# First layer of a four-layer network: inverse norms and softmax reciprocals spread over the channels by HBM reads instead of matmuls

## The chip, the cores and the metric

One core of a Trainium2 chip runs the whole network in one launch, in float32. The engines are named as the profile names them: PE (TensorE matmuls; PEld its weight loads), DVE (VectorE), ACT (ScalarE), POOL (GpSimd) and SP (SyncE, which here issues the DMAs of this layer). The metric is the device time in microseconds (us), the median of several executions of the same program. A time is given against the profiled execution where it is read from the trace.

## What is computed

The network has four layers over x of shape (2, 512, 64, 64). The change touches the first one, attention with a 3x3 neighbourhood and pooled keys, run on the normalised input of each image. Per image there are N = 4096 tokens, C = 512 channels in 8 heads of 64. Cut to what matters:

```
q = heads(xf @ W_q + b_q)
q_norm = q / max(norm(q), 1e-12)                  # per head and token
q_scaled = (q_norm + query_embedding) * softplus(temperature)
k_l, v_l = split(xf @ W_kv + b_kv)
k_l = k_l / max(norm(k_l), 1e-12)                 # per head and token
k_local, v_local = the 9 neighbours (3x3, zero padded) of k_l, v_l
attn_local = sum over channels of q_scaled * k_local        # 9 per head and token
attn_pool  = q_scaled . l2norm(k_pool)                      # 256 pooled keys
a_local, a_pool = split(softmax(concat(attn_local, attn_pool)))
lt = q_norm . learnable_tokens + learnable_bias + a_local
out = (sum over 9 of lt * v_local + a_pool . v_pool) @ W_proj + b_proj
```

Two quantities exist once per head and token and must multiply all 64 channels of the head: the inverse norm of k and q, and the reciprocal of the softmax's sum (on the pooled part; `lt` for the nine neighbours carries it already). The channels lie on the partitions, so each has to be spread over 64 partitions. How that is done is what the change changes.

## The kernel before

`Net.layer0` opens the pools and runs the class `Local`: SBUF `wp`, DRAM `yp`, and PSUM with five banks for `mm` (the method `bank`), one for `tap` and two for `qs`. Work is cut into units. A unit is 1024 tokens (16 rows of the image, two blocks of 512) of one chunk of 128 channels (two heads); 4 units by 4 chunks are 16 units an image.

`run` goes through turns i = -4 to 16. In turn i it makes generators and interleaves them step by step (`in_turn` takes one step of each in a round):

- `norms`: the inverse norms of what was projected in the turn before. Four matmuls sum the squares of four streams (k and q, two blocks each) over the heads (L2048), ACT copies to SBUF (L2051), four transposes (L2055), small DVE operations for the inverse root (L2062 to L2070), four transposes back (L2076) and an ACT copy to `rows` (L2078).
- `tap_products(i+1)`: two ACT copies of the scaled queries to PSUM (L2133), then nine DVE multiplies of 128x1024, one for each neighbour, with the keys `kx` (L2138), in a ring of three buffers `prods`.
- `attend(i)`: scores against the pooled keys (L2183), exponentials on ACT (L2187), values (L2193) with an ACT copy (L2195), sums of exponentials on POOL (L2198), then the softmax's sums on PE (L2205, L2209), two DVE reciprocals of 128x256 (L2230), the multiply of `el` by them (L2233) and the addition of the learned term (L2234). The rows are written to HBM (`rows`, L2237), and read back broadcast over the channels as "taps", one per neighbour, by `fetch_tap` (L2247: two DMAs of 256 KB, one a head).
- `weigh(i-1)`: the reciprocal, spread by two K=2 matmuls (L2260), multiplies the pooled output (DVE, L2263). Then for each of nine taps: ACT copies the tap to PSUM (L2270), DVE multiplies with the values `vx` (L2273), POOL adds to the output (L2277). The result goes to HBM as `yd` (L2283). The taps have a ring of three buffers.
- `tap_sums(i+1)`: matmuls that sum each product over the head (L2151), and the exponential (ACT, L2166) which gives `el`.
- `projections`: k of unit i+4, q of unit i+3 and v of unit i+1: a block is four matmuls of 128x512, one per chunk of input channels (L133; the trace has two records for each matmul; k and q stand at the end of the steps), with ACT taking out k or q with its bias (L2014) and its square (L2016), v with its bias (L2122).
- `normed`: the spread of the inverse norms by four K=2 matmuls (L2090), DVE multiplies k into `kx` and q in place (L2098), then `learned`: four matmuls with the learned tokens (L2111), ACT adds their bias (L2114) and scales the queries (L2116).
- in the last turns `fetch_output` and `output`: the projection `W_proj`, with the reload of `yd`.

The generators give the order in which operations are written down; the framework then puts them in an order per engine and sets the waits for data and buffers. Every engine takes its instructions in that order. All DMAs of this layer are issued by SP, in order as well: a DMA that must wait for data or a buffer holds those behind it.

Quantities per turn in the middle of an image: 21 DMAs issued by SP; 18 ACT copies of taps; nine products and nine tap multiplies in two halves on DVE.

## Time and profile before

| | |
|---|---|
| median of 11 executions | 5453.23 us |
| lowest, highest | 5436.49, 5470.63 us |
| the profiled execution | 5456.72 us |
| its span | 5454.8 us, so 1.9 us lie around it |
| mean granted PE clock | 0.969 |
| instructions | 51666 |
| one turn in the middle of the first layer (9 per image) | 45.86 us |
| the nine of image 1, 446.06 to 858.78 | 412.72 us |
| the nine of image 2, 3147.28 to 3560.01 | 412.73 us |

How to read it: the span is the profiled execution from first to last instruction. A row of groups gives a line of the kernel, engine, operation, its operands by the program's names (tiles that are parts of a larger buffer carry its name: `big` and `late` hold most of this layer), the shape, how many there were, then busy time, the mean of one in ns, and the idle time of the engine just before them with what ended most of it. A row of the timeline gives start, duration, engine, line and operation, and in brackets the idle time before it with the releaser. Windows give the busy time of each engine in a stretch. A count of matmul records can be a few per cent short. The 512-column matmuls of one block L133 that follow each other show 3.70 us as a row, and the next work of PE starts 3.63 us after its start.

The change touches no line outside the first layer.

### The profile page before, as it was taken

To read this page: it belongs to the slowest core of one execution; us is meant where nothing else is said; L and a number is where in the kernel's file an instruction comes from. 1 tells how busy PE (TensorE), PEld (TensorE's weight loads), DVE (VectorE), ACT (ScalarE), POOL (GpSimd) and SP (SyncE) were. 2 spreads that over 40 slices of the span, in tenths; PEclk is the share of its full clock that TensorE was granted. 3 is DMA by queue.
4 is the path that set the end of the run, shared out by engine and by line. 5 is a ranking of instruction groups with operands and counts; after the bars stand their busy time and mean duration, and the time that the engine had idled before them with its cause. 6 is when DMAs were issued, how large, how long until landed. Compare 5 with 4: busy or idle time off the path is not lost. (4 is left out here: it accounts for less than half of the span.)

```text
span 5454.8 us, 51666 instructions
## 1 busy us (share of the span) xinstructions
PE 5161.4 (95%) x18891; PEld 2251.2 (41%) x18891; DVE 3144.1 (58%) x3918; ACT 1793.5 (33%) x3409; POOL 1802.9 (33%) x1198
## 2 busy tenths in 40 slices
PE   7999999999988899999999999998999889999998
PEld 3423333554333444544344233335543334445443
DVE  3256667745679633565532666666456895334565
ACT  1245555233212233212212555542432132332221
POOL 0025556401310045444400355553012101554443
PEclk9999999999989999899999999999999899998999
DMA  3024445500000000211110344455000000000111
GB/s 141 2 63 122 127 126 160 147 18 24 1 1 0 1 0 1 84 34 56 51 55 2 83 126 128 125 152 149 1 24 0 1 0 1 1 8 20 37 36 42
DMA packets 113564, 293.27 MB, mean 54 GB/s; under 512 B 17235, under 2 KB 30035, under 8 KB 111253
## 3 DMA queue, kind: packets, MB, share of 16 engines
q1 hardware_dynamic: 113300, 289.88, 18.4%
q8 instruction: 151, 2.47, 0.2%
q14 instruction: 113, 0.92, 0.1%
HBM read 241.32 MB, written 48.50 MB: 53 GB/s over the span
## 5 line engine op out<-in xcount | busy, mean ns | idle before, releaser
L133 PE MATMUL mm<-big,w 128*128 128x512 f32 x2560 | 1189.6, 609 | 5.0 <-DVE late L2230 4.9
L133 PEld LDWEIGHTS mm<-big,w 128*128 128x128 f32 x2560 | 468.2, 192 | 688.5 <-issue 592.5
L2277 POOL TENSOR_TENSOR late<-late,big 128x1024 f32<-128x1024 f32 x192 | 454.6, 2368 | 304.6 <-DVE big L2273 296.1
L1265 POOL TENSOR_TENSOR total<-prob 128x512 f32<-128x512 f32 x128 | 159.6, 1269 | 761.7 <-ACT prob L1262 761.7
L1182 PE MATMUL acc<-big,dg 128*128 128x512 f32 x704 | 317.5, 608 | 58.8 <-DVE big L697 28.3
L1624 POOL TENSOR_SCALAR qf_sum<-qf,ksum_ratio 128x512 f32<-128x512 f32 x128 | 198.8, 1562 | 508.9 <-ACT qf L1674 351.6
L1437 POOL TENSOR_TENSOR big<-big 128x512 f32<-128x512 f32 x224 | 277.4, 1270 | 238.5 <-ACT big L1428 238.5
L2198 POOL TENSOR_TENSOR late<-late 128x512 f32<-128x512 f32 x128 | 160.6, 1276 | 490.7 <-ACT late L2187 450.9
L697 DVE TENSOR_TENSOR big<-big 128x3968 f32<-128x3968 f32 x72 | 308.8, 4290 | 6.9 <-ACT big L698 0.9
L2273 DVE TENSOR_TENSOR big<-big,mm 128x512 f32<-128x512 f32 x384 | 254.4, 679 | 85.7 <-ACT mm L2270 82.6
L1428 ACT ACTIVATE big<-mm,ed 128x256 f32<-128x256 f32 x512 | 193.9, 488 | 279.1 <-DVE top L1424 251.4
L2270 ACT COPY mm<-big 128x512 f32<-128x512 f32 x384 | 221.1, 594 | 170.9 <-DMA big<-rows 131.9
L1362 PE MATMUL mm<-proj,k 64*128 64x256 f32 x2048 | 270.5, 394 | 0.9 <-ACT k L1329 0.9
L1282 DVE RECIPROCAL recip<-psD 128x512 f32<-128x512 f32 x64 | 214.9, 3357 | 87.2 <-PE psD L1279 87.2
L1655 PE MATMUL mm<-k,w 128*128 128x512 f32 x512 | 241.1, 610 | 14.6 <-DVE k L1648 14.6
L1583 DVE TENSOR_REDUCE tops<-mm 128x2 f32<-128x512 f32 x256 | 161.4, 684 | 160.9 <-PE mm L1362 160.4
L1262 ACT ACTIVATE prob<-mm 128x512 f32<-128x512 f32 x256 | 132.0, 605 | 364.4 <-PE mm L1259 359.2
L1362 PEld LDWEIGHTS mm<-proj,k 64*128 64x128 f32 x2048 | 207.2, 188 | 105.9 <-issue 90.1
L2138 DVE TENSOR_TENSOR prod<-qs,big 128x1024 f32<-128x1024 f32 x192 | 230.4, 1215 | 30.9 <-PE tap L2151 29.1
L2277 POOL TENSOR_TENSOR late<-late,tap 128x1024 f32<-128x1024 f32 x96 | 226.6, 2361 | 63.6 <-DVE tap L2273 44.9
L133 PE MATMUL mm<-big,big 128*128 128x512 f32 x512 | 238.8, 629 | 0.0
L2151 PE MATMUL tap<-prod,cst 128*32 128x512 f32 x768 | 226.4, 612 | 9.6 <-DVE prod L2138 9.5
(364 smaller groups left out, 8295.8 us busy)
## 6 DMA issues: line engine op xcount, KB each, us to landing
big<-rows SPq DMA_DIRECT2D x384, 256.0 KB
tap<-rows SPq DMA_DIRECT2D x192, 256.0 KB
yd<-late SPq DMA_DIRECT2D x32, 512.0 KB
lost_all<-lost SPq DMA_DIRECT2D x128, 128.0 KB
out<-big SPq DMA_DIRECT2D x64, 256.0 KB
big<-in_W_kv SPq DMA_DIRECT2D x8, 1024.0 KB
rows<-late SPq DMA_DIRECT2D x64, 128.0 KB
big<-yd SPq DMA_DIRECT2D x16, 512.0 KB
```

The source lines that it names most:

```text
L133: self.nc.tensor.matmul(ps, w[:, kc, :], X[:, kc, blk * TB:(blk + 1) * TB], start=(kc == 0), stop=(kc == KC - 1))
L697: nc.vector.tensor_tensor(o, a, b, ALU.max)
L1182: nc.tensor.matmul(accs[b], dg, src[:, b * TB:(b + 1) * TB], start=(j == 0), stop=(j == 6))
L1282: nc.vector.reciprocal(r, psD)
L1362: nc.tensor.matmul(pS[h][i][:, t, :], k[lo:lo + HD, tok:tok + P], proj[lo:lo + HD, :], start=True, stop=True)
L1437: nc.gpsimd.tensor_tensor(a, a, part, ALU.add)
L1655: nc.tensor.matmul(ps, self.wo[:, kc, oc * P:(oc + 1) * P], qs[:, kc, :], start=(kc == 0), stop=(kc == KC - 1))
L2138: self.nc.vector.tensor_tensor(self.prods[k % 3].rearrange("p (y x) -> p y x", x=W), qs, self.kx[:, y + dy:y + dy + self.UY, dx:dx + W], A ...
L2151: nc.tensor.matmul(ps[32 * q:32 * q + 32, :], self.cst[:, C_TAPW + 16 - 2 * k:C_TAPW + 48 - 2 * k], self.prods[k % 3][:, j * TB:(j + 1) * ...
L2270: nc.scalar.copy(ps, part)
L2273: nc.vector.tensor_tensor(part.rearrange("p (y x) -> p y x", x=W), self.vx[:, y:y + self.UY // 2, dx:dx + W], ps.rearrange("p (y x) -> p y ...
L2277: nc.gpsimd.tensor_tensor(out, out, self.taps[k % 3], ALU.add)
```

## The change

The reciprocals and inverse norms are no longer spread by matmuls; they are written to HBM and read back broadcast over 64 partitions each, as the taps are. In detail:

1. `norms` ends with two DMAs that write the inverse norms (8 KB each) to a DRAM tile `roots`, and four DMAs that read them back broadcast over all channels (256 KB each; queries into two of the `sq` tiles, keys into `kraw`; queries first). `normed` copies them to PSUM by ACT (four copies; in place of the K=2 matmuls L2090), and DVE multiplies as before. ACT writes k, not yet normalised, straight into `kx`, and the multiply is in place there. Queries come before keys, and `learned` right after the queries.
2. The softmax's reciprocal is read from a row of `el` (row 20 of each half), where the multiply by the reciprocal leaves it: there the exponential is exp(0) = 1, and the learned term is 0. `fetch_tap` takes it as a tenth tap with number 0; `weigh` copies it to PSUM by ACT (two copies, in place of the K=2 matmuls L2260) and multiplies the pooled output with it in its first step. The ring of taps now turns with 10u + i.
3. `norms` and `normed` stand after `projections` in the list of stages; `norms` has two steps fewer, `normed` waits six steps instead of five, `fetch_output` seven instead of three.

```diff
--- before.py
+++ after.py
@@ -1715,6 +1715,7 @@
 
         self.yd = yp.tile([P, KC, N], F32, name="yd")
         self.wd = yp.tile([3, P, KC, C], F32, name="wd")
+        self.roots = cycle([yp.tile([2, 4, TB], F32, name=f"roots{i}") for i in range(2)]).__next__
         self.rows = cycle([yp.tile([P // 2, self.UT], F32, name=f"rows{i}") for i in range(2)]).__next__
 
         R = W + 2
@@ -1749,12 +1750,13 @@
         self.vp = new([P, 2, C], "vp")
         self.qn = new([P, self.UT], "qn")
         self.w3 = new([P, 3, KC, P], "w3")
-        self.sq = [new([P, TB], f"sq{i}") for i in range(4)]
+
+        self.squares = new([P, 4, TB], "sq")
+        self.sq = [self.squares[:, i, :] for i in range(4)]
         self.half = new([P, 32], "mhalf32")
         self.wide = new([P, NT, P], "wide")
         self.qb = new([P, KC], "qe_scaled")
         self.bias = {i: new([P, KC], "b_" + i) for i in "qkv"}
-        self.raw = {"k": self.kraw, "q": self.qn}
         self.w, self.lt, self.el, self.out = {}, {}, {}, {}
         load = lambda w, src: nc.sync.dma_start(w, src.rearrange("(kc p) o -> p kc o", p=P))
         load(self.w_sr, d["W_sr"])
@@ -1791,7 +1793,7 @@
         for i in range(-4, units + 1):
             k, q, ahead, u, before = (unit(i + n) for n in (4, 3, 1, 0, -1))
             streams, ended = [], []
-            stages = [self.norms(streams, ended)]
+            stages = []
             if ahead is not None:
                 stages.append(self.tap_products(ahead))
             if u is not None:
@@ -1804,7 +1806,7 @@
             values = ([ahead] if i >= self.UN - 1 and ahead is not None
                       else {-4: [0], -3: [1, 2], -2: [3]}.get(i, []))
             stages.append(self.projections(k, q, values, streams))
-            stages.append(self.normed(ended))
+            stages += [self.norms(streams, ended), self.normed(ended)]
             if i < -2:
                 stages.append(islice(heads, 12 if i == -4 else None))
             if i == units - 3:
@@ -1945,7 +1947,7 @@
 
     def fetch_output(self):
 
-        for _ in range(3):
+        for _ in range(7):
 
             yield
         for kc in range(KC):
@@ -2010,8 +2012,13 @@
                 return
             b = self.bias[which][:, u // self.UN:][:, :1]
             ps = self.projected(which, u % self.UN * 2 + j)
-            part = self.raw[which][:, j * TB:(j + 1) * TB]
-            nc.scalar.activation(part, ps, AF.Identity, bias=b)
+            if which == "k":
+                y = 1 + u % self.UN * self.UY + j * self.UY // 2
+                part = self.kx[:, y:y + self.UY // 2, 1:W + 1]
+            else:
+                part = self.qn[:, j * TB:(j + 1) * TB]
+            nc.scalar.activation(part, ps.rearrange("p (y x) -> p y x", x=W) if which == "k" else ps,
+                                 AF.Identity, bias=b)
             sq = self.sq[len(streams)]
             nc.scalar.activation(sq, ps, AF.Square, bias=b)
             streams.append((which, u, j, part, sq))
@@ -2042,7 +2049,6 @@
         before, self.pending = self.pending, streams
         if not before:
             return
-        yield
         ps = self.bank()
         for s in range(4):
             nc.tensor.matmul(ps[32 * s:32 * s + 32, :], self.cst[:, C_E32:C_E32 + 32],
@@ -2070,40 +2076,46 @@
             nc.vector.scalar_tensor_tensor(dst, a, 1.5, y, ALU.add, ALU.mult)
         yield
         yield
-        yield
         ps = self.bank()
         for t in range(NT):
             nc.tensor.transpose(ps[:, t * P:(t + 1) * P], self.wide[:, t, :], self.net.ident)
         rows = wp.tile([P, TB], F32, name="n_rows")
         nc.scalar.copy(rows, ps)
-        ended += [(s, rows[32 * s:32 * s + 2, :], *a) for s, a in enumerate(before)]
+
+        roots = self.roots()
+        for h in range(2):
+            nc.sync.dma_start(roots[h], rows[h:P:32, :])
+        for s in reversed(range(0, len(before), 2)):
+            dst = (self.kraw if before[s][0] == "k"
+                   else self.squares[:, 2:].rearrange("p s n -> p (s n)"))
+            for h in range(2):
+                nc.sync.dma_start(dst[h * HD:(h + 1) * HD, :].rearrange("p (s n) -> p s n", s=2),
+                                  bcast(roots[h, s:s + 2], 0, HD))
+            ended += [(dst[:, j * TB:(j + 1) * TB], *before[s + j]) for j in range(2)]
         yield
 
     def normed(self, ended):
 
         nc = self.nc
-        for _ in range(5):
-            yield
-        for which in "kq":
-            mine = [(e, self.bank()) for e in ended if e[2] == which]
-            for (s, rows, *_), ps in mine:
-                nc.tensor.matmul(ps, self.cst[32 * s:32 * s + 2, C_ROW:C_ROW + P], rows, start=True,
-                                 stop=True)
-            for (_, _, _, u, j, part, _), ps in mine:
-                out = part
+        for _ in range(6):
+            yield
+        for which in "qk":
+            mine = [(e, self.bank()) for e in ended if e[1] == which]
+            for (root, *_), ps in mine:
+                nc.scalar.copy(ps, root)
+            for (_, _, u, j, part, _), ps in mine:
                 if which == "k":
-                    y = 1 + u % self.UN * self.UY + j * self.UY // 2
-                    out = self.kx[:, y:y + self.UY // 2, 1:W + 1]
-                    part, ps = (a.rearrange("p (y x) -> p y x", x=W) for a in (part, ps))
-                nc.vector.tensor_tensor(out, part, ps, ALU.mult)
-            yield
-        if mine:
-            self.learned(mine[-1][0][3])
-        yield
+                    ps = ps.rearrange("p (y x) -> p y x", x=W)
+                nc.vector.tensor_tensor(part, part, ps, ALU.mult)
+            yield
+            if which == "q":
+                if mine:
+                    self.learned(mine[-1][0][2])
+                yield
 
     def learned(self, u):
 
-        nc, cc, qn = self.nc, u // self.UN, self.raw["q"]
+        nc, cc, qn = self.nc, u // self.UN, self.qn
         ps = self.bank()
         for j in range(2):
             for g in range(2):
@@ -2235,49 +2247,47 @@
         self.spread = self.rows()
         for j in range(2):
             nc.sync.dma_start(self.spread[:, j * TB:(j + 1) * TB], el[j * HD:(j + 1) * HD, :])
-        self.fetch_tap(0)
-        yield
-        self.fetch_tap(1)
-        yield
-
-    def fetch_tap(self, k):
-
-        at = 32 * (k % 2) + 2 * k
+        self.fetch_tap(u, 0)
+        yield
+        self.fetch_tap(u, 1)
+        yield
+
+    def fetch_tap(self, u, i):
+
+
+        at = 32 * ((i - 1) % 2) + 2 * (i - 1) if i else 20
+        t = self.taps[(10 * u + i) % 3]
         for h in range(2):
-            self.nc.sync.dma_start(self.taps[k % 3][h * HD:(h + 1) * HD, :],
-                                   bcast(self.spread[at + h], 0, HD))
+            self.nc.sync.dma_start(t[h * HD:(h + 1) * HD, :], bcast(self.spread[at + h], 0, HD))
 
     def weigh(self, u):
 
         nc = self.nc
         cc, y0 = u // self.UN, u % self.UN * self.UY
-        out, R = self.out.pop(u), self.recip
-        self.fetch_tap(2)
-        yield
-        banks = [self.bank() for _ in range(2)]
-        for j, ps in enumerate(banks):
-            q = slice(64 * j, 64 * j + 2)
-            nc.tensor.matmul(ps, self.cst[q, C_ROW:C_ROW + P], R[q, :], start=True, stop=True)
-        for j, ps in enumerate(banks):
-            o = out[:, j * TB:(j + 1) * TB]
-            nc.vector.tensor_tensor(o, o, ps, ALU.mult)
-        for k in range(9):
-            dy, dx = divmod(k, 3)
-            parts = [self.taps[k % 3][:, j * TB:(j + 1) * TB] for j in range(2)]
+        out = self.out.pop(u)
+        for i in range(10):
+            if i + 2 < 10:
+                self.fetch_tap(u, i + 2)
+            t = self.taps[(10 * u + i) % 3]
+            parts = [t[:, j * TB:(j + 1) * TB] for j in range(2)]
 
             banks = [self.bank() for _ in range(2)]
             for ps, part in zip(banks, parts):
                 nc.scalar.copy(ps, part)
+            dy, dx = divmod(i - 1, 3)
             for j, (ps, part) in enumerate(zip(banks, parts)):
+                if i == 0:
+                    o = out[:, j * TB:(j + 1) * TB]
+                    nc.vector.tensor_tensor(o, o, ps, ALU.mult)
+                    continue
                 y = y0 + dy + j * self.UY // 2
                 nc.vector.tensor_tensor(
                     part.rearrange("p (y x) -> p y x", x=W),
                     self.vx[:, y:y + self.UY // 2, dx:dx + W],
                     ps.rearrange("p (y x) -> p y x", x=W), ALU.mult)
-            nc.gpsimd.tensor_tensor(out, out, self.taps[k % 3], ALU.add)
-            if k + 3 < 9:
-                self.fetch_tap(k + 3)
-            if k < 8:
+            if i:
+                nc.gpsimd.tensor_tensor(out, out, t, ALU.add)
+            if i < 9:
                 yield
         lo = u % self.UN * self.UT
         nc.sync.dma_start(self.yd[:, cc, lo:lo + self.UT], out)
```

## The prediction

> **What bounds the kernel now.** I read the page's first part (busy time by engine) first, then the busy time of each engine in windows of one turn, then the groups and the order of time within one turn.
>
> ```profile
> PE 5161.4 (95%) x18891; PEld 2251.2 (41%) x18891; DVE 3144.1 (58%) x3918; ACT 1793.5 (33%) x3409; POOL 1802.9 (33%) x1198
> ```
>
> TensorE (PE) is the engine to relieve over the whole span. The chain of waits names only about a fifth of the span and no line of this layer, so it doesn't help. The first layer is what the change touches; cut at the starts of the matmuls of L2260, each turn in its middle looks like this (time, then busy time by engine, clock, DMA share, GB/s):
>
> ```profile
> 491.91:537.77 45.86, 45.74 (x166) 14.75 (x165) 31.60 (x50) 25.85 (x45) 26.21 (x13) 1.00 0.48 126
> 537.77:583.63 45.86, 45.74 (x167) 14.75 (x165) 31.60 (x50) 25.82 (x45) 26.20 (x13) 1.00 0.46 121
> ...
> 858.78:1100.00 241.22, 223.58 (x662) 109.40 (x660) 176.46 (x271) 85.18 (x151) 126.44 (x61) 0.97 0.54 151
> 225.00:351.32 126.32, 121.33 (x406) 43.72 (x401) 46.96 (x85) 45.05 (x71) 5.01 (x4) 0.96 0.07 19
> 351.32:446.06 94.74, 87.33 (x307) 26.71 (x305) 61.72 (x100) 50.07 (x87) 52.43 (x26) 0.98 0.46 117
> ```
>
> In the nine steady turns of an image (446.06 to 858.78, and again in image 2: 18 in all) PE idles 0.12 of 45.86 us; DVE is at 69%, ACT 56%, POOL 57%. So a matmul taken away there is worth its full time as long as nothing makes PE wait, and every wait of PE costs its full length. Around them PE has holes: 5.0 us before 351.32, 7.4 in the first turns, 17.6 in the last ones.
>
> The groups of the steady turns (busy, mean ns, idle before):
>
> ```profile
> L2138 DVE TENSOR_TENSOR prod<-qs,big 128x1024 f32<-128x1024 f32 x54 | 65.0, 1216 | 12.5 <-PE tap L2151 11.7
> ...
> L2230 DVE RECIPROCAL late<-mm 128x256 f32<-128x256 f32 x18 | 30.3, 1726 | 3.7 <-PE mm L2209 3.7
> L2090 PE MATMUL mm<-n_rows,cst 2*128 2x512 f32 x72 | 20.3, 640 | 0.0
> ...
> L2263 DVE TENSOR_TENSOR late<-late,mm 128x512 f32<-128x512 f32 x18 | 12.3, 683 | 91.7 <-PE mm L2260 91.7
> ```
>
> DVE idles 10.2 us at each turn's head (91.7 over nine) until PE reaches L2260. That is slack of DVE, no loss of time: PE works through it.
>
> And the place that the change disturbs, in order of time (start, duration):
>
> ```profile
> 515.46 1.07 PE L2209 MATMUL mm<-late,cst 64*64 64x512 f32 x4
> ...
> 516.46 3.70 PE L133 MATMUL mm<-big,w 128*128 128x512 f32 x8
> 516.58 3.37 DVE L2230 RECIPROCAL late<-mm 128x256 f32<-128x256 f32 x2 [0.41 <-PE mm L2209]
> ...
> 522.05 1.23 DVE L2138 TENSOR_TENSOR big<-qs,big 128x1024 f32<-128x1024 f32 x1 [0.18 <-PE tap L2151]
> ...
> 524.98 1.22 DVE L2138 TENSOR_TENSOR prod<-qs,big 128x1024 f32<-128x1024 f32 x1
> ```
>
> After the sums DVE takes the reciprocals, and the next unit's first two tap products (L2138) start 5.6 and 8.5 us after the sums' end. PE asks for them only at 541.5 (a turn after its first tap matmuls, L2151, of 495.68), because both q blocks, scores, a v block and values stand ahead. The wait is covered.
>
> [...] a pair with K=2 (L2260, L2090) holds PE 1.05 us, a full pair of L133 0.91 (a block of eight 3.63 from start to start). [...] Here the pair of writes of the rows (issued 521.90, 1.10 us) is followed by the first read at 524.90: about 1.9 us of SP standing still. [...]
>
> **The change part by part.**
>
> *Removed.* Six K=2 matmuls a turn (four of L2090, two of L2260), three pairs of 1.055 us: 3.17 us of PE a turn. In the order that the changed program has once built, the tap matmuls also stand in fewer groups, of five, four, four, one and four; from groups of four at 1.0, five at 1.8 and a lone one at 0.98 I estimate 5.78 instead of 6.76: 0.98 saved. PE's work in a steady turn: 45.74 - 3.17 - 0.98 = 41.6.
>
> *Moved: norms behind projections.* With this order the steady turn ends: k0, sums, k1, learned matmuls (L2111 of before), the first four tap matmuls of the next unit, q0, q1. These four now stand ahead of q0, with 3.63 + 0.88 = 4.5 us of PE's work between them and the sums. On DVE their data come behind the reciprocals: 3.51 from the sums' end to the end of the pair, two tap multiplies (0.61, 0.6), the multiply of el (0.6), product 0 (1.13), the addition (0.6), product 1 (1.22), 0.05 for the hand-over: 8.3 us. PE waits 8.3 - 4.5 = **3.8 us a turn** where it waited for nothing. q0 can't pass: PE takes its instructions in order. Two smaller waits by the same counting: product 7 behind tap multiplies ahead of v1, 1.0; k0's bank behind a multiply of tap 5, 0.4.
>
> *Added: the inverse norms through HBM.* Transposes' end to multiplied queries: ACT copy 0.75, first write's issue and the second's 1.1, landing 1.2 (the 8 KB write of L1603, issued 2281.63 with 1.11, let L1616 go at 2283.39), two reads 1.1, landing 3.5 (a tap read issued 503.30 to 504.39 served ACT at 507.94), two ACT copies 1.1 (0.594 each, 0.52 apart), DVE 0.7: 9.5 us. PE between has scores 1.05, a tap matmul 0.98, values 1.87, k0 3.63, sums 2.9 = 10.4, and k1's bank needs the query multiply. About 1 us of slack. While the root copies wait, ACT is held in order: k0's Identity and Square, the query scaling and copies of qs stand behind; those gate DVE's products and PE's banks. On SP the write's landing holds taps 7 to 9 back. SP issues 29 instead of 21 DMAs of 0.55 a turn (16 of 46 us). Bytes go from about 5.6 to 7.1 MB a turn (taps 9 to 10 pairs of 256 KB, four root reads of 256 KB), so the DMA share from 0.48 to about 0.62; 0.72 was seen at 885 to 930. Half a tap read of 256 KB now stands just ahead, about 0.9 us at the 280 GB/s of the busiest stretches. Bounds of the cost: 0 (covered) to 3 us a turn (a landing half as long again, and SP's wait for the write as long as that of the rows). I take 0.5: the slack of 1 less the 0.9 leaves nothing, with a little jitter.
>
> *Added: four ACT copies for the norms and two for the tenth tap.* 6 x 0.594 = 3.6 us on ACT, 25.8 to 29.4 of 46: hidden, except that they are in order. DVE has the same number of multiplies; k is now multiplied in place, a strided write by ACT at 0.689 against 0.687: nothing.
>
> *The recip as tap 0.* It frees DVE from L2260, the 10.2 us of idleness, but DVE wasn't the bound.
>
> *Sum of a steady turn.* 41.6 + 3.8 + 1.0 + 0.4 + 0.5 = 47.3 against 45.86: +1.45, x18 = +26.
>
> *The rest of the layer, per image.* The four turns before unit 0's attention save the K=2 pairs where they exist: 2.8 + 1.0 + 0.9 + 0.6 = 5.3 (the learned matmuls wait there about 1.9 for the round trip, since only k0 and k1, 7.3, cover 9.2). Turns 1 and 2 have no values block, PE holes of 7.4 already, and save 2.8 each. Turn 12 has no k: its reciprocal comes behind the root copies and two products, +4; turn 13 +0.5. The last weighing has ten taps in three buffers with nothing beside it: one more round of copy, multiply, add and read, +2.5 (3.5 at most). -5.3 - 5.6 + 4 + 0.5 + 2.5 = -4, x2 = -8.
>
> Total +26 - 8 = +18. Against the profiled execution 5456.7 (span 5454.8 and 1.9 around it) that is 5475; that execution lies 3.5 above the median 5453.2, so 5471 for a median.
>
> **The rivals.**
>
> A, faster: PE doesn't wait for the products. Place: the four tap matmuls ahead of q0. It decides if DVE delivers product 1 within about 5.5 us of the sums, or if PE comes there late for another reason. Then a turn is 41.6 + 1.4 = 43.0, -2.9 x 18 = -51, with the -8: about 5394. For it: DVE has 14 us of idleness a turn, and the groups L2230 and L2138 keep their lengths. Against it: 3.37 of reciprocal and two products of 1.2 alone are 5.8, in a fixed order with four more operations between. I give 0.20.
>
> B, slower: the root reads come later. It decides from the point where the round trip, 9.5 by my count, passes the 10.4 of PE's work ahead of k1; from there PE loses all that is beyond, since ACT holds the query copies in front of k0's eviction. At the upper bound of 3 us for my 0.5: +2.5 more a turn, +45: about 5516. For it: 29 issues, one queue, write before read. Against it: the reads are short and the share stays under the 0.72 seen. 0.20.
>
> C, a wash: the roots cost nothing (0 for my 0.5), and the first two of the four tap matmuls run while product 1 is made, so that 3.3 of the 3.8 is left: 41.6 + 3.3 + 1.4 = 46.3, +0.44 x 18 = +8, and the -8 cancels it: 5453, with 11 to either side. It lies near my case; I doubt it only because everything on SP and ACT must be on time. 0.16.
>
> That the change doesn't do what it says I exclude: the matmuls of both lines are gone from the built program.
>
> **How the numbers follow.** My case 0.44, A 0.20, B 0.20, C 0.16. Time 5471. The measurement can tell about 0.2% (11 us) from no change. Slower: mine and B but for mine's low end, 0.61; within: C and a little of mine, 0.17; faster: A and the low end of C, 0.22. Range 5395 (A's value) to 5525 (B with its spread); mine alone 5455 to 5492.
>
> **What would show it.** Right: PE idle before the tap matmuls, released by DVE's products, near 3.8 us in every steady turn; a steady turn of about 47.3; ACT idle before the new root copies under 2 us with PE hardly waiting. If PE waits for the query multiply at k1, B holds. If steady turns are near 43, A. Wrong in the sum: if the first or last turns move by more than 5 us each.

## The result and the profile after

The changed kernel takes 5541.26 us (median of 8, 5529.23 to 5547.98) against 5455.27 for the kernel before (31 executions): a ratio of 1.0155, interval 1.0144 to 1.0166. It is slower by 86 us, as forecast in sign, but outside the range of 5395 to 5525. Its profiled execution takes 5540.13 us.

The busy times by engine on the page after. PE has 40 us less to do, and the span is 83.5 us longer, so PE now idles or waits for over 120 us more:

```profile
PE 5121.3 (92%) x18507; PEld 2244.9 (41%) x18507; DVE 3178.0 (57%) x3918; ACT 1883.8 (34%) x3601; POOL 1810.1 (33%) x1198
```

To see where, both traces were cut at the start of the last matmuls of the softmax's sums (L2209 before, L2221 after), once a turn. Image 1, in us:

| stretch | before | after | difference | predicted |
|---|---|---|---|---|
| up to the sums of turn 3 | 469.60 | 464.82 | -4.8 | -10.9 |
| turns 3 to 11, eight steady turns | 366.86 | 394.32 | +27.5 | +11.6 |
| turns 11 to 15, the last ones | 182.01 | 204.79 | +22.8 | +4.5 |
| sum | 1018.47 | 1063.93 | +45.5 | +5.2 |

The last column leaves out the ninth steady turn, which these marks cut in two (+1.45), and the last weighing (+2.5). The first stretch also holds work from before the layer's first square of a projected block (L2016 before, L2023 after; at 193.76 and 195.76). Counted from there it takes 275.84 and 269.06, or -6.8. In image 2 the steady turns go from 366.87 to 397.47 (+30.6), as in image 1, but the last ones from 189.82 to 202.49 (+12.7). So the loss at the end is seen in both images, while its size is less certain: the kernel before alone differs by 7.8 between its two.

Three of the steady turns after, as windows (time, busy time of PE, PEld, DVE, ACT, POOL, granted clock, DMA share, GB/s):

```profile
464.82:512.02 47.20, 43.55 (x154) 14.39 (x153) 33.69 (x52) 29.36 (x54) 26.47 (x14) 1.00 0.62 159
512.02:561.91 49.89, 46.23 (x154) 15.22 (x152) 32.05 (x50) 27.78 (x51) 26.47 (x14) 0.93 0.56 147
610.73:658.71 47.98, 43.55 (x155) 14.40 (x153) 33.40 (x51) 29.60 (x54) 26.45 (x14) 1.00 0.60 154
```

Two things are to be seen. Where the clock is 1.00, a turn is PE's work of 43.55 and about 4 us of waits. Where it is 0.93, the same matmuls keep PE busy for 2.7 us longer. Over the eight turns PE is busy 362.8 us and waits 31.5: per turn 43.55 of work, 1.8 for the clock, 3.9 of waits, 49.3 in all.

The order of time on PE after the sums of one turn (start, duration, and in brackets the wait and its releaser):

```profile
658.71 1.07 PE L2221 MATMUL mm<-late,cst 64*64 64x512 f32 x4
659.71 3.70 PE L133 MATMUL mm<-big,w 128*128 128x512 f32 x8
663.34 1.07 PE L2123 MATMUL mm<-qn,big 128*32 128x512 f32 x8
666.22 1.05 PE L2163 MATMUL tap<-big,cst 128*32 128x512 f32 x4 [1.81 <-DVE big L2150]
668.90 1.92 PE L2163 MATMUL tap<-prod,cst 128*32 128x512 f32 x4 [1.63 <-DVE prod L2150]
670.75 9.07 PE L133 MATMUL mm<-big,w 128*128 128x512 f32 x16
```

The first four tap matmuls of the next unit wait 1.81 and 1.63 us for tap products 0 and 1, as the prediction had it (3.44 for 3.8). But the two q blocks behind them (q0 and q1; k0 and k1 are the two of k) take 9.0 us where two blocks take 2 x 3.63 = 7.26. The windows of the same stretch show why; the clock is the last but two:

```profile
661.00:664.00 3.00, 3.00 (x14) 0.92 (x12) 3.00 (x4) 2.23 (x4) 1.28 (x1) 1.00 0.82 194
664.00:669.00 5.00, 1.56 (x10) 0.28 (x8) 5.00 (x6) 3.88 (x7) 2.69 (x1) 0.88 0.71 153
669.00:674.00 5.00, 5.00 (x8) 1.60 (x9) 5.00 (x8) 1.18 (x2) 2.62 (x2) 0.50 0.75 199
674.00:679.00 5.00, 5.00 (x12) 2.24 (x11) 1.82 (x2) 1.26 (x2) 2.10 (x1) 0.93 0.79 244
```

PE is active for 1.56 of the 5 us from 664 to 669; from then to 674 the granted clock is 0.50. The longest single wait here is 1.81 us, and 2.0 in all eight turns.

In this trace waits of nearly the same length go with a loss of clock in one turn and with none in another. In the clock records of this execution the stretches of half clock begin on one grid of 3.41 us and, but for one, last whole steps of it: 3.41 or 6.83 us in the eight turns. In the six of the eight turns where the clock falls, PE idled 2.15 to 2.36 us of the step just before; here it worked 1.05 of the 3.41 us from 664.43 to 667.84, and the clock was at half until 674.67. In the turns from 464.82 and 610.73, which stayed at 1.00, the waits are nearly as long (1.79 and 1.6 us), but a border of the grid lies between the two, so that no step has more than 1.79 us of idleness. No run tested whether this is the cause.

In the last turns the wait is another. Turn 13 to 14 after, in order of time on SP, ACT, DVE and PE:

```profile
964.72 1.11 SPq L2249 DMA_DIRECT2D rows<-late  x2
...
970.27 0.33 SPq L2293 DMA_DIRECT2D yd<-late  x1
970.65 0.43 SPq L1968 DMA_DIRECT2D w<-yd  x1
...
971.25 1.32 SPq L2261 DMA_DIRECT2D big<-rows  x2
...
979.39 1.11 ACT L2276 COPY mm<-big 128x512 f32<-128x512 f32 x2 [10.38 <-DMA big<-rows]
...
980.01 1.28 DVE L2281 TENSOR_TENSOR late<-late,mm 128x512 f32<-128x512 f32 x2 [6.73 <-ACT mm L2276]
...
982.48 1.91 PE L2163 MATMUL tap<-big,cst 128*32 128x512 f32 x2 [7.19 <-DVE big L2150]
```

The reciprocal, tap 0, is read at 971.25, behind the rows' landing and the store and reload of `yd`. Of this time SP stood 4.4 us for POOL's last addition, which the store needs. From the read's issue to ACT's copy another 8.1 us pass, where a tap read in a steady turn before served ACT 4.6 us after its issue began (503.30 to 507.94); the DMA share is 1.02 from 973 to 984. Which of the two weighs more, the late issue or the busy DMA engines, wasn't tried. ACT stands 10.38 us before its copy, and DVE 6.73 before the multiply L2281. Behind DVE's multiply in order is a tap product, and PE waits 7.19 us for it.

In the steady turns DVE idles about as long before this multiply, as in the turn from 658.71, but not for the read:

```profile
682.13 0.69 DVE L2281 TENSOR_TENSOR late<-late,mm 128x512 f32<-128x512 f32 x1 [6.31 <-ACT mm L2276]
```

There ACT takes the copy only after it has emptied the q blocks, and PE works in these blocks meanwhile.

### The profile page after: what moved, and what is told of

Read it like the earlier page. It is cut to its first block, busy times and chain, and to the rows that moved or that the text cites. A ratio compares the mean times of both kernels' runs of the same rounds, so it can differ in the third digit from the quotient of the medians.

```text
span 5538.3 us, 51520 instructions
## 1 busy us (share of the span) xinstructions
PE 5121.3 (92%) x18507; PEld 2244.9 (41%) x18507; DVE 3178.0 (57%) x3918; ACT 1883.8 (34%) x3601; POOL 1810.1 (33%) x1198
## 5 line engine op out<-in xcount | busy, mean ns | idle before, releaser
L133 PE MATMUL mm<-big,w 128*128 128x512 f32 x2560 | 1204.8, 617 | 20.8 <-DVE big L2284 10.1
L2276 ACT COPY mm<-big 128x512 f32<-128x512 f32 x428 | 246.2, 596 | 178.4 <-DMA big<-rows 104.6
```

Source lines behind the costliest of these rows:

```text
L133: self.nc.tensor.matmul(ps, w[:, kc, :], X[:, kc, blk * TB:(blk + 1) * TB], start=(kc == 0), stop=(kc == KC - 1))
L2276: nc.scalar.copy(ps, part)
```

## The experiments

All medians in us; the steady turn is the mean of the eight between the sums of turns 3 and 11 of image 1, the last turns are those from 11 to 15; both come from the profiled execution of each. The runs were made in six groups, each beside the kernel before, whose median there lies between 5444 and 5457. Runs of different groups are therefore better compared by their ratios than by their medians.

| run | median | ratio to before (interval) | steady turn | last turns |
|---|---|---|---|---|
| before | 5455.27 | | 45.9 | 182.0 |
| after | 5541.26 | 1.0155 (1.0144 to 1.0166) | 49.3 | 204.8 |
| pinned | 5532.55 | 1.0130 (1.0106 to 1.0153) | 48.5 | 204.7 |
| recip_only | 5430.89 | 0.9956 (0.9933 to 0.9979) | 43.9 | 189.8 |
| roots_only | 5491.31 | 1.0058 (1.0035 to 1.0080) | 48.5 | 190.3 |
| learned_twice | 5527.65 | 1.0126 (1.0101 to 1.0151) | 47.9 | 204.3 |
| pinned_keys_sbuf | 5529.18 | 1.0135 (1.0118 to 1.0152) | 48.7 | 206.0 |
| recip_order | 5476.21 | 1.0042 (1.0025 to 1.0059) | 46.0 | 187.9 |
| norms_front | 5722.41 | 1.0494 (1.0476 to 1.0512) | 55.6 | 200.4 |
| fetch_early | 5535.99 | 1.0150 (1.0130 to 1.0170) | 49.3 | 201.9 |
| late_k2 | 5471.52 | 1.0050 (1.0033 to 1.0067) | 46.5 | 190.5 |
| short_recip | 5531.79 | 1.0151 (1.0134 to 1.0167) | 50.9 | 192.4 |
| recip_mostly | 5461.91 | 1.0028 (1.0020 to 1.0035) | 43.8 | 201.5 |
| pinned_keys_last | 5467.10 | 1.0043 (1.0029 to 1.0058) | 45.2 | 205.9 |
| after_ring | 5504.73 | 1.0112 (1.0090 to 1.0134) | 49.0 | 191.6 |
| recip_ring | 5410.54 | 0.9928 (0.9913 to 0.9943) | 44.4 | 179.8 |
| order_only | 5448.51 | 0.9995 (0.9985 to 1.0004) | 45.8 | 183.8 |
| edges_ring | 5453.69 | 0.9999 (0.9989 to 1.0009) | 45.0 | 197.1 |

### The parts alone

**recip_only**: part 2 put into the kernel before (`fetch_tap` and `weigh` as changed, all else as before).

```diff
-        self.fetch_tap(0)
+        self.fetch_tap(u, 0)
...
-                nc.tensor.matmul(ps, self.cst[q, C_ROW:C_ROW + P], R[q, :], start=True, stop=True)
```

> The kernel before with part 2 alone: the reciprocal is read back as a tenth tap, L2260's matmuls go; norms and their K=2 matmuls stay. Theory (the waits come from the tap products placed ahead of q0, which this order doesn't have; the end of the layer loses because the tenth tap heads the weighing): steady turns 44.8, -1.06 x 18 = -19, and +10 to +20 an image in its last turns: 5455 to 5475. Rival (part 2 costs nothing at the end): 5425 to 5440.

Measured 5430.89, faster than before, and in the rival's range. A steady turn as a window:

```profile
637.17:680.86 43.69, 43.67 (x162) 14.60 (x161) 32.01 (x51) 26.56 (x47) 25.95 (x14) 1.00 0.56 144
```

PE hardly waits, at full clock. The turn is 2 us under before, not 1.06: the tap matmuls stand on PE in five groups (1, 6, 3, 4, 4) for six before (5, 1, 4, 1, 4, 3). In the turn from 537.77 before, a lone one holds PE 0.98 us, and a group of three or four about 1.0, so I estimate another microsecond for one group less. The last turns lose 7.8 us in image 1, where 10 to 20 were expected, and gain 3.2 in image 2, so by themselves they don't settle whether the tenth tap costs there. recip_ring, below, does: with these turns alone weighed as before, the time falls by another 20 us. So the rival's number came true for another reason, a steady turn that gains twice what the theory gave it.

**roots_only**: the changed kernel with `fetch_tap` and `weigh` of before (parts 1 and 3).

```diff
-        self.fetch_tap(u, 0)
+        self.fetch_tap(0)
...
+                nc.tensor.matmul(ps, self.cst[q, C_ROW:C_ROW + P], R[q, :], start=True, stop=True)
```

> The changed kernel without part 2: the reciprocal is spread by the two K=2 matmuls of before, nine taps; the roots go through HBM. In its order the two matmuls of tap product 0 alone stand ahead of q0. Theory (wait and clock): one wait of about 2 us a turn, and where the clock follows it 1 to 3 us more: steady turns 45.7 to 48.5; total 5440 to 5500; if a wait of 2 us doesn't lower the clock, the low end. Rival (the roots' chain is the cost): PE waits at k1 for the query multiply, and the time is near the changed kernel's, 5520 or more.

5491.31, within the theory's range. Waits of up to 2.1 us at the tap matmuls and at the query multiply, 25 us from 460 to 860. So the reciprocal alone gains, and parts 1 and 3 together cost.

**order_only**: the move of part 3 alone (`norms` and `normed` behind `projections`, with their steps of before), in the kernel before.

```diff
-            stages = [self.norms(streams, ended)]
+            stages = []
...
-            stages.append(self.normed(ended))
+            stages += [self.norms(streams, ended), self.normed(ended)]
```

> The kernel before with norms and normed moved behind projections (part 3), nothing else. Theory (the move alone costs PE nothing but the grouping of tap matmuls, which stays): within 12 of before. Rival (the move itself makes PE wait): 5480 or more.

No difference: the move costs nothing by itself. **recip_order** is part 2 and the move (the changed kernel with `norms`, `normed` and their K=2 matmuls of before):

```diff
...
-                nc.scalar.copy(ps, root)
...
+                nc.tensor.matmul(ps, self.cst[32 * s:32 * s + 2, C_ROW:C_ROW + P], rows, start=True,
+                                 stop=True)
...
```

> The changed kernel with the K=2 matmuls of before for the norms in place of the roots: part 2 and the move of norms and normed behind projections (part 3), without part 1. Theory (the roots through HBM push the multiplies of keys and queries behind the sums; the order alone doesn't): near the run of part 2 alone, 5431, within 15. Rival (the order is the cause): 5480 or more, with PE waiting for DVE after the sums.

5476.21: neither. PE hardly waits (0.5 us a turn on average, clock 1.00), but the tap matmuls stand in six groups again, and one is interleaved with the norms' matmuls. The steady turn is 2.1 us longer than in recip_only, 1.7 of it PE's work: in the turn from 612.58 the tap groups take 1.1 us more, and the norms' four sums of squares, with the tap matmul between them, 1.8 for 1.0. The way in which the framework groups the tap matmuls is worth as much as a pair of K=2 matmuls taken away.

The parts don't add up one by one. The move costs nothing alone, but some 45 us on top of part 2 (recip_only to recip_order); the roots through HBM, with the order of steps that came with them, cost another 65 (recip_order to the changed kernel).

### The steady turns: where PE's claim on late data stands

**pinned**: one edge of order in the changed kernel.

```diff
+            if which == "q":
+                self.last_q = nc.cur_bb.bb.instructions[-1]
...
-            sums(k)
+            if k == 0:
+                with self.net.tc.issue_after(self.last_q):
+                    sums(0)
+            else:
+                sums(k)
```

> The changed kernel with one added edge of order: the first tap matmul of the next unit is queued on PE behind the last q projection, as it stood before the change. Everything else, the roots' DMAs too, stays. Theory (PE waits 3.4 us a turn for tap products 0 and 1, and the granted clock falls to half for some us after these waits): both go, steady turns of about 43 us (45.74 - 3.17 and a few tenths) at clock 1.00 where they are 49.3 on average now, so 18 x 6.3 = 113 us less: about 5430. Rival 1 (the low clock has another cause, such as more DMA or ACT work): only the waits go, 18 x 3.4 = 61: about 5480, clock still 0.93 to 0.97. Rival 2 (the root reads are late): the wait moves to k1 behind the query multiply, 5500 or more.

5532.55: the number is in rival 2's range, but no cause of the three holds. The wait for the products is gone, and another, not at k1, took its place:

```profile
622.94 0.59 ACT L2107 COPY mm<-big 128x512 f32<-128x512 f32 x1 [1.60 <-DVE big L2290]
624.56 1.28 DVE L2111 TENSOR_TENSOR big<-big,mm 128x512 f32<-128x512 f32 x2
625.29 6.34 PE L133 MATMUL mm<-big,w 128*128 128x512 f32 x8 [3.73 <-DVE big L2111]
```

The second q block, q1, waits 3.73 us for a PSUM bank. ACT had filled it with key roots (L2107), and DVE comes to their multiply (L2111) only after the reciprocals, `el`, three products and taps. The block then takes 6.3 us instead of 3.6: the low clock again (0.57 on average from 625.29 to 631.56). Over the eight turns this wait is 23.1 us, 2.9 a turn; 3.7 is the longest.

**learned_twice**: more work for PE, with which the framework puts the tap matmuls behind the q blocks by itself.

```diff
-        for j in range(2):
-            for g in range(2):
-                q = 2 * j + g
...
+        for q in 2 * [0, 1, 2, 3]:
+            j = q // 2
...
```

> The changed kernel with the four learned matmuls of each turn done twice: 0.89 us more PE work a turn. With this the framework puts the tap matmuls of the next unit behind q0, q1 and the scores. Theory: more work and less time: steady turns about 43.9 (43 and 0.89) at clock 1.00: 18 x 5.4 = 97 less, about 5445, some 16 above the run with the edge of order. Rival (the order isn't the cause): 5541 + 16 to 28 = 5560 or more.

5527.65: 14 us less than the changed kernel with 0.9 us more of PE's work a turn, not the 97 expected. In the turn from 560.8 q1 waits 1.9 us for the key multiply, and k0 0.7 for a tap multiply; over the eight turns the waits for the key multiply are 17.7 us. The direction fits, though at the edge of the noise; the size was that of a theory without the banks.

**pinned_keys_sbuf**: pinned, and no banks for key roots.

```diff
-            mine = [(e, self.bank()) for e in ended if e[1] == which]
+            mine = [(e, self.bank() if which == "q" else e[0]) for e in ended if e[1] == which]
             for (root, *_), ps in mine:
-                nc.scalar.copy(ps, root)
+                if which == "q":
+                    nc.scalar.copy(ps, root)
```

> The run with the edge of order, and in it the keys are multiplied by their roots straight from SBUF: no ACT copies of the key roots, no two PSUM banks held by them. In the run with the edge alone q1 waited 3.7 us a turn for a bank that a key root's copy held until DVE had multiplied, behind reciprocals, el, three tap products and taps, 15 us of DVE work without a gap. Theory (this burst on DVE after the sums, through banks, is what PE waits for; the order of the tap matmuls only chose the place): the wait at q1 goes, and with it the half clock after it; steady turns 43 to 44, about 90 less than 5532: 5435 to 5455. Rival (any bank will do: the next one held by a tap multiply takes its place): 5500 or more.

The rival holds: 5529.18. The waits from 460 to 860 are for tap multiplies now, and DVE has more to do:

```profile
615.67 2.85 DVE L2112 TENSOR_TENSOR big<-big 128x512 f32<-128x512 f32 x1
```

With one operand in PSUM the multiply takes 0.68 us; here it took 1.23 and 2.85 in the turn from 606.62. The 30 of these 64 multiplies beside which POOL runs nothing take 0.63 to 0.70 us, so it isn't SBUF alone that makes them long; 28 of the 34 that overlap an instruction of POOL take over 1 us, and 27 of these end 0.55 us after that instruction does. So most of these lasted until POOL's addition was over. This makes the run no clean test of the banks: DVE is busy for 2.2 us more a turn than in pinned (278.2 and 260.4 in the eight).

**pinned_keys_last**: pinned, and the key roots' copies take their banks only after the q blocks.

```diff
+            if which == "k":
+                yield
+                yield
+                yield
...
+                if which == "k":
+                    with self.net.tc.issue_after(self.last_sq):
+                        nc.scalar.copy(ps, root)
```

> The run with the edge of order (tap matmuls behind the q blocks), with a second edge: ACT's copies of the key roots are queued behind the last square of q, so that they take no PSUM banks while the q blocks wait for one. The roots go through HBM as in the changed kernel. In the run with one edge q1 waited 3.7 us for such a bank. Theory (two claims on PE ahead of or in the q blocks, the tap products and the banks that root copies hold, are what the road through HBM brings; DVE's burst is as long in the run with late K=2 matmuls, 5472, without harm): the wait at q1 goes, steady turns 43 to 44.5 at clock 0.99 or more, 5430 to 5460. Rival (as where the keys were read from SBUF, tap copies hold the next bank): turns 47 or more, 5500 or more.

5467.10, 74 us under the changed kernel (some 61 by the ratios), 7 above the theory's range. PE's waits from 460 to 860, and a steady turn:

```profile
PE mm L133 <- DVE big L2300: 10.1, 10, 1.4
PE mm L133 <- DVE tap L2300: 5.3, 6, 1.4
PE mm L133 <- DVE qn L2121: 3.7, 3, 1.9
```

```profile
605.18:650.87 45.69, 42.81 (x154) 13.75 (x152) 33.02 (x50) 29.86 (x53) 26.53 (x14) 1.00 0.63 162
```

The longest wait is 1.9 us and the clock stays at 1.00. With the roots still going through HBM, the steady turn is under before (45.2 for 45.9), though above the theory's 44.5, and the whole kernel is still 0.4% slower than before. The profiled execution, at 5492, is the longest of its five, so its last turns may say too much.

**late_k2**: the roots' copies replaced by K=2 matmuls at their place in the changed kernel.

```diff
...
-                nc.scalar.copy(ps, root)
+                s, r = root
+                nc.tensor.matmul(ps, self.cst[32 * s:32 * s + 2, C_ROW:C_ROW + P], r, start=True,
+                                 stop=True)
```

> The changed kernel with its order of stages, steps and queries first kept, but the four ACT copies of roots read from HBM replaced by the four K=2 matmuls of before at the same place in the program; no root DMAs. In its order the query pair stands ahead of the sums, the key pair between q0 and q1. Theory A (what costs is that the multiplies of queries and keys come at and after the sums, into DVE's burst, with banks held until then; HBM only makes them late): PE waits 2 to 4 us a turn at q1 or the scores and loses clock after it; turns 47 to 50, 5490 to 5540. Theory B (the road through HBM itself costs: ACT held in order for root reads, SP for the write, so taps come late into the burst): no waits over 1 us, turns 45 to 46, 5450 to 5480.

5471.52, in theory B's range, though the turn of 46.5 is above it. This is all that PE waits for from 460 to 860:

```profile
PE tap L2156 <- DVE big L2143: 4.3, 8, 0.6
PE tap L2156 <- DMA tap<-rows: 0.8, 1, 0.8
```

DVE's work after the sums is much the same burst here: in the turn from 599.86 the reciprocals run until 4.1 us after the sums' end, the first three products until 9.8, and the key multiplies begin at 11.0. So a burst of this length need not hurt. But the order is another, too: DVE makes product 0 right behind the reciprocals, and of the tap matmuls only one, of product 0, stands ahead of q0; its other one and those of product 1 come behind it.

```profile
606.16 1.05 PE L2156 MATMUL tap<-big,cst 128*32 128x512 f32 x2 [0.60 <-DVE big L2143]
```

So this run doesn't separate the road through HBM from the place of the claims. With pinned and pinned_keys_last it says where the burst hurts: where PE's order asks for its products early, or where ACT fills banks long before DVE empties them. Here the matmul that spreads the keys takes its bank at 610.77 and DVE begins to empty it at 611.93; in pinned ACT's copies took theirs from 620.74 on, and DVE came at 624.56.

**short_recip**: DVE's reciprocals replaced by short multiplies.

```diff
-            nc.vector.reciprocal(self.recip[:, part], psD[:, part])
+            nc.vector.tensor_scalar(self.recip[:, part], psD[:, part], 0.004, None, ALU.mult)
```

> The changed kernel with the two reciprocals of 128x256 replaced by two multiplies by a constant of the same shape (the softmax isn't normalised: that part is left out), which DVE does in about 0.7 us in all instead of 3.4. Theory (DVE's burst after the sums is too long for PE's cover[...]): 2.7 us less wait a turn and the half clock gone, turns 44 to 45 at clock 0.99 or more: 90 less, 5440 to 5460. Rival 1 (only the wait goes, the clock stays low for other reasons): 5490. Rival 2 (DVE's length doesn't matter): 5520 or more.

5531.79, as rival 2 had it, but it doesn't decide: the framework put a tap matmul of the next unit even ahead of k1, straight behind the sums, and there it waits:

```profile
PE tap L2163 <- DVE big L2150: 35.9, 8, 5.4
```

It agrees that the place of the claim counts; whether the reciprocals' length does, with the place kept, stays open.

**norms_front**: norms and normed ahead of all other stages.

```diff
-            stages = []
+            stages = [self.norms(streams, ended), self.normed(ended)]
...
-            stages += [self.norms(streams, ended), self.normed(ended)]
```

> The changed kernel with norms and normed ahead of the other stages of a turn instead of behind projections; the roots still go through HBM, all else as changed. In its order the learned matmuls stand ahead of the sums again. Theory (the burst after the sums): key and query multiplies leave it, so PE's waits after the sums shrink to about 1 us or less; turns 43.5 to 46; 5440 to 5490. Rival (the roots' round trip is the cost wherever it stands): PE waits for the query multiply ahead of the sums instead, 5510 or more.

5722.41, the rival's side, with another wait than the rival's: k0 stands 9 us for a tap multiply. The trace points to SP and ACT:

```profile
648.64 0.49 SPq L2260 DMA_DIRECT2D big<-rows  x1
651.28 1.11 SPq L2091 DMA_DIRECT2D sq<-roots  x2
652.45 1.23 SPq L2091 DMA_DIRECT2D big<-roots  x2
653.72 0.59 SPq L2260 DMA_DIRECT2D big<-rows  x1
661.01 1.11 ACT L2275 COPY mm<-big 128x512 f32<-128x512 f32 x2 [6.40 <-DMA big<-rows]
```

The second half of a tap's read stands behind SP's wait of 2.1 us for the write of the roots and behind the four root reads, and the DMA share is 1.08 from 655 to 661; ACT waits 6.40 us for this tap. Here the road through HBM costs on the one queue, as rival B of the prediction feared, but by late taps and not by late roots.

### The last turns

**fetch_early**: `fetch_output` waits three steps.

```diff
-        for _ in range(7):
+        for _ in range(3):
```

> The changed kernel with the fetch of the output weights three steps into its turn, as before, instead of seven. Theory: the last turns' loss (22.8 us an image between the sums of turn 11 and turn 15) has its cause elsewhere: within 8 of 5541. Rival (the later fetch, 1.5 MB in a busy stretch, makes the loss): 10 to 30 less.

5535.99, within the theory's 8 us, of two executions only; the last turns keep 201.9 us. The fetch isn't what makes the loss.

**recip_mostly**: part 2 alone with the last units weighed as before.

```diff
+        return 1 if u > KC * self.UN - 5 else 0
...
+        if first:
...
+                nc.tensor.matmul(ps, self.cst[q, C_ROW:C_ROW + P], R[q, :], start=True, stop=True)
...
-        for i in range(10):
+        for i in range(first, 10):
```

> The run of part 2 alone, in which the last four units of an image are weighed as before (K=2 matmuls, nine taps). With part 2 alone the four turns from the sums of turn 11 to those of turn 15 took 189.8 us for 182.0 before. Theory (the tenth tap's read heads the weighing where little is left beside it): the 7.8 us are saved twice: 5415 to 5422. Rival (the loss in these turns has another cause): 5428 to 5440.

5461.91, worse by 31. The ring of tap buffers still turned with 10u + i, so that a unit of nine taps asked for a buffer one step too early, and SP, in order, stood from 882 to 904 us but for `yd` and the output's weights:

```profile
880.92 1.18 SPq L2253 DMA_DIRECT2D big<-rows  x2
890.66 0.33 SPq L2298 DMA_DIRECT2D yd<-late  x1
891.59 0.33 SPq L1966 DMA_DIRECT2D w<-yd  x1
897.33 0.81 SPq L1952 DMA_DIRECT2D sq<-in_W_proj  x2
904.36 1.09 SPq L2253 DMA_DIRECT2D big<-rows  x2
```

**recip_ring** and **after_ring** do the same to part 2 alone and to the changed kernel, with the ring counted on:

```diff
+    def tap(self, u, i):
+        whole = KC * self.UN - 4
+        n = 10 * u + i if u < whole else 10 * whole + 9 * (u - whole) + i - 1
+        return self.taps[n % 3]
```

recip_ring:

> Part 2 alone, the last four units weighed as before, the ring counted on without a gap. Theory: 182 to 186 us from the sums of turn 11 to those of turn 15 where part 2 alone takes 189.8: 5416 to 5426. Rival (as in the first run of the kind, the loss there has nothing to do with the ring): 5440 or more.

after_ring:

> The changed kernel in which the last four units of an image are weighed as before (reciprocal by K=2 matmuls, nine taps), the ring of tap buffers counted on without a gap. Theory (in turns 13 to 16 the reciprocal's read, the first in ACT's and DVE's queues, is late by the rows' landing and the reload of yd; exponentials and tap products stand behind it, and PE has no q blocks to cover this): the sums of turn 11 to those of turn 15 take 188 to 193 us instead of 204.8, about 12 to 16 an image: 5510 to 5518. Rival (the root reads or the fetch make the loss): 5530 or more.

recip_ring takes 5410.54, below the range expected, and is the fastest kernel of the study: 0.72% under before, and its last turns take 179.8 us. after_ring takes 5504.73, also below its range, with last turns of 191.6 for 204.8. In image 2 the edit takes 10.7 us off these turns in part 2 alone (186.6 to 175.9) and 12.3 in the changed kernel (202.5 to 190.2), much as in image 1. Both say that the tenth tap makes most of the loss there. That it is its late read, and not the added round of copy and multiply, rests on the waits shown above.

**edges_ring**: after_ring's edit in pinned_keys_last.

> The run with both edges of order (tap matmuls and key roots' copies behind the q blocks), and the last four units weighed as before, the ring counted on. The roots and the other reciprocals still go through HBM. Theory (the two causes are separate and add up): 5467 less the 36 that the ring edit brought in the changed kernel: 5425 to 5440, under before. Rival (they overlap): 5450 or more.

5453.69, no different from before, and above the theory's range. Whether the two causes overlap isn't decided. By the medians the ring edit brought 13 us here and 36 in the changed kernel; by the ratios, each to the kernel before in its own group, it brought 0.44% here and 0.43% there. What is shown is that the two edges and the ring edit together bring the changed kernel back to the time of before. The last turns keep 197.1 us; there PE waits once 6.4 us for the reciprocals and once 4.0 for the query multiply. What else is late in those turns with the roots through HBM wasn't taken apart.

## Why the prediction was wrong

- **Right: the wait for products.** 3.8 us a turn were predicted; it is 3.44, at the instructions named. What pinned added: without it a wait nearly as long, 2.9 us a turn, follows at PE's next claim.
- **Wrong by omission: the granted clock.** The sum of a steady turn has no term for it. It is 1.8 us a turn over the eight turns, some 32 us over 18. The views before showed clock 1.00 in turns without a gap, and 0.97 in the stretch with gaps; that was shown and not read. This and the next one are the two large errors of the steady turn.
- **Wrong in size: PE's work in a steady turn.** Put at 41.6, it is 43.55. The estimate of 0.98 saved by fewer groups of tap matmuls failed: in the turn from 610.73 the groups take 7.7 us, not 5.78, because the wait cuts one group of four in two of about 1.0 each, and another of four takes 1.85.
- **Too large: the other waits.** 1.0, 0.4 and 0.5 were counted; measured are about 0.5 in all. Rival B, the query roots late at k1, is 0.80 and 0.58 us in two of the turns and hardly seen in the others: a root read served ACT 5.0 us after its issue began (702.20 to 707.20), and the whole way from the transposes' end to the multiplied queries took 10.1 us in that turn for the 9.5 counted. In the steady turn these errors sum to +2.0 over the 47.3 predicted, 36 us over 18.
- **Wrong: the last turns, a wait put at almost nothing.** Against the +4 for turn 12 and +0.5 for turn 13 stand 22.8 us in image 1 and 12.7 in image 2. Left out: the reciprocal comes as a DMA at the head of ACT's and DVE's order where before it came from PE, and the q blocks that hide this end with turn 12. after_ring takes 13 and 12 of it back. The step "It frees DVE from L2260, the 10.2 us of idleness, but DVE wasn't the bound" looked at DVE's load, and not at what stands behind DVE's first instruction.
- **Too good: the first turns**, -6.8 for -10.9, counted from the layer's first square. Which term is off wasn't looked into.
- Of the rivals, A (no wait for the products) is shown false in the changed kernel. Its 5394 is reached by no version. Part 2 alone, without the roots, has turns of 43.9 us, near A's 43.0, since PE waits for nothing there; that is A's condition in a kernel that lacks parts 1 and 3.

## What to carry to other kernels

When a bound engine's small instructions are traded for transfers, ask where the freed engine's next claim on late data stands in its order, and which scarce buffer the transferred value occupies from its landing to its use. Taking away one such wait only showed the next, until both were gone (pinned 5533, pinned_keys_last 5467). A gap in PE is to be priced with the clock that may be lost after it, here about half its length again (1.8 us for 3.9 of waits a turn); and take the half of a change that gains (recip_ring, 5411) by itself.

## What the hardware showed

- In the changed kernel half clock (0.50) came in steps of a grid of 3.41 us, and in the steady turns after a step in which PE idled at least 2.15 us; up to 1.79 it kept 1.00. So two waits of 1.8 and 1.6 us within 4.5 us went with 3.4 or 6.8 us of half clock where most of both fell into one step, and with none in the two turns where they didn't. That idleness isn't all of it: in the same execution the clock also fell at 189.98, after a step with 1.03 us of idleness, and at 2268.70, after one with none (PE busy for 3.40 of 3.40 us). In recip_ring it fell at 596.59 after a step with one wait of 1.0 us and a pair of K=2 matmuls. What else counts stays open.
- A DVE multiply of 128x512 took 0.68 us with an operand in PSUM (L2263 before), and 0.63 to 0.70 with both in SBUF while POOL did nothing. While POOL added, the one with both in SBUF took up to 2.90 us and as a rule ended 0.55 us after POOL's addition (pinned_keys_sbuf). The additions of the learned term in the changed kernel (L2246, both operands in SBUF) show the same: 6 beside which POOL did nothing took 0.68 us, and the 26 that began while POOL added took 1.71 to 2.25 and ended 0.55 after it. The multiply of `el` just ahead (L2245), of which 26 began 0.2 us before POOL did, took 0.68.
- Tap matmuls of 32 columns cost by the group: one 0.98 us, three or four about 1.0, five 1.8 (before, turn from 537.77), six 1.85 (recip_ring, 662.05); one group of four took 1.85 (changed kernel, 643.09).
